# Last attention stage: the second pair's heads swap rows and key orders, the second pair's results move to a bank of their own, and the key-sum products move behind the next item's scores

## The chip, the cores and the metric

The kernel runs on one core of one Trainium2 chip. The metric is device time in microseconds (us) for one execution, lower is better. The engines are named as in the profile: PE is TensorE (matrix products and transposes), PEld its weight loads, DVE is VectorE, ACT is ScalarE, POOL is GpSimd, SP is SyncE. Each engine works through its own queue in order and waits on semaphores that the other engines raise.

## The reference, cut to what matters

The whole network is two layers on x of shape (2, 1024, 256): adapter, linear attention, mixture of experts, then sparse or dense attention, the attention that is changed here, an adapter and a feed-forward part. The changed part is local attention with 16 heads of 64 in blocks of 128 queries. A block sees its own block of keys and both neighbours (within 127 positions), and 64 "side" keys more, each the sum over 16 tokens of the input, projected:

```python
def _L1_attn_ref(x, Wq, Wk, Wv, Wo):        # x (2, 1024, 256); H, dh = 16, 64
    bl = 128; nb = L // bl; G = L // 16     # 8 blocks, 64 side keys
    q = einsum('bld,dhk->blhk', x, Wq) / sqrt(dh)
    k, v = einsum('bld,dhk->blhk', x, Wk), einsum('bld,dhk->blhk', x, Wv)
    g = einsum('bld,lg->bgd', x, one_hot(arange(L) // 16))
    side_k, side_v = einsum('bgd,dhk->bghk', g, Wk), einsum('bgd,dhk->bghk', g, Wv)
    k_cat = concat([3 blocks of k, side_k]); v_cat = concat([3 blocks of v, side_v])
    logits = einsum('bnqhd,bnkhd->bnhqk', qb, k_cat) + bias      # 0 or -1e9 outside |rel| <= 127
    m = maximum(logits.max(-1), 0)
    probs = exp(logits - m) / (exp(logits - m).sum(-1) + exp(-m))
    y = einsum('bnhqk,bnkhd->bnqhd', probs, v_cat)
    return einsum('blhk,hkd->bld', y, Wo)
```

## The kernel before, in words

Everything is float32. `attn1` handles the two sequences (b) one after the other. For each it computes the keys into `kT` (line 1577), 64 rows for the even head of a pair of heads and 64 rows for the odd one. The key blocks and the side keys stand in `kT` in an order that `KEYS` gives: `KEYS[0]` for the upper 64 rows, `KEYS[1]` for the lower 64. Then it computes the values (`v`) and the summed values (`sv`).

`attn1_heads` does the attention itself. Its unit is an item: one block n of 128 queries and two pairs of heads, m and m+1, so four heads. There are 8 blocks by 4, that is 32 items for a sequence, 64 in all. Blocks 0 and 7 are the edge blocks (two key blocks instead of three); the others are called inner here. An item passes five steps:

- `scores`: for each pair four products of 64 rows by 64 columns (two heads, two halves of the queries) into a tile `ps` of two banks. DVE merges the two neighbour blocks for an inner block (`copy_predicated`, lines 1691 and 1698: one copy of 128x128 and two of 64x64), then one instruction per head (1707) subtracts, masks and finds the extreme into `pe` and `nm`. ACT takes the exponentials in place (`exps`, 1726), pair 0 and pair 1 apart.
- `turn`: PE transposes `pe`, eight blocks into the banks `pt0` and `pt1` (1757) and two blocks with the side keys into `pts` (1758). Into the same `pts` go two transposes with the reciprocals of the item before (`recip`, 1737). ACT copies `pt0` (1763) and `pts` (1774) to SBUF, DVE copies `pt1` with its two masks (1765).
- `invert`: the reciprocal of the denominators (1742), widened by ACT (1744).
- `sums`: four products of the side weights with `sv` into `py` (1793), 64x64 each.
- `values`: twelve products (eight at an edge) of 128 rows by 64 columns into `py` (1810), accumulated on the sums. DVE then multiplies by the reciprocals into `yT` (1822).

`py` is one bank of four slots of 128 columns; an item uses two of them, the next item the other two. Queries for two blocks (`queries`, 1653) and the output product for two blocks (`output`, 1832) are interspersed, three and four times per sequence. The steps overlap: in round i the loop at line 1839 issues scores of item i, sums of item i-2, turn of item i-1, the second exponentials of item i, invert of i-1, and values of i-2. A scheduler sets the order in each engine's queue; `behind` adds an order between two instructions of one engine without a wait. PSUM's eight banks are all used: `ps` twice two, `pt0`, `pt1`, `pts`, `py`.

Of the kernel before, what the change touches and what calls it, by code (L numbers as in the profile page):

```python
# [18 lines left out]
P = 128  # L19
# [1496 lines left out]
def attn1(k, ci, x):  # L1516
# [7 lines left out]
    with tiles(tc, name="a1r", bufs=1) as rp:  # L1524
# [13 lines left out]
        for b in range(B):  # L1538
            kT = rp.tile([P, 8, S + 4 * (G + 2)], F32, name="kT")
            for i in range(2):  # L1540
                for at in KEYS[i].sums:
                    nc.gpsimd.memset(kT[64 * i : 64 * i + 64, :, at - 1 : at + G + 1 : G + 1], 0.0)
            v = rp.tile([P, NB, 1024], F32, name="v")

            sv = rp.tile([P, 2, 8, 64], F32, name="sv")
            with ExitStack() as st:
# [15 lines left out]
                for m in range(8):  # L1562
                    ms = slice(m * P, (m + 1) * P)
                    for half in range(2):
                        ts = slice(b * S + half * CK, b * S + (half + 1) * CK)
                        pq = pp.tile([P, CK], F32, name="pq", bufs=3)
                        for c in range(2):
                            nc.tensor.matmul(pq, lhsT=wk[:, c, ms], rhs=ci[:, c, ts], start=c == 0, stop=c == 1)  # L1568
                        gs = slice(half * G // 2, (half + 1) * G // 2)
                        nc.vector.reduce_sum(sk[:, m, gs], pq.rearrange("p (g t) -> p g t", t=16), axis=AX.X)  # L1570
                        for i in range(2):
                            hp = slice(64 * i, 64 * i + 64)
                            for n0, n1 in KEYS[i].runs(4 * half, 4 * half + 4):
                                at, w = KEYS[i].at[n0], (n1 - n0) * P
                                o = (n0 - 4 * half) * P
                                copy = nc.vector.tensor_copy if i else nc.scalar.copy
                                copy(kT[hp, m, at : at + w], pq[hp, o : o + w])
                    if beside:
                        next(beside[m // 4])
                    if m % 4 == 3:  # L1580
                        for i in range(2):
                            hp = slice(64 * i, 64 * i + 64)
                            for at in KEYS[i].sums:
                                nc.gpsimd.tensor_copy(kT[hp, m - 3 : m + 1, at : at + G], sk[hp, m - 3 : m + 1])
                for half in range(2):
                    hs = slice(half * CK, (half + 1) * CK)
                    for j in range(NB):
# [30 lines left out]
def attn1_heads(k, b, x, ci, kT, v, sv, masks, rp, sp, pp, yp):  # L1618
# [22 lines left out]
    def behind(ins, other):  # L1641

        how = mybir.DependencyInfo(mybir.DependencyClass.NoSync, mybir.DependencyReason.DATA)
        k.tc.add_manual_dep(ins.ins, other.ins.name, how, reason="order")

    def queries(n):

# [14 lines left out]
    def scores(it):  # L1662
# [2 lines left out]
            queries(0)  # L1665
        if m == 4 and n % 2 == 1 and n + 1 < NB:
            queries(n + 1)
        views = window(n)
# [4 lines left out]
        for pair in range(2):  # L1673
            ps = pp.tile([P, 2, CK], F32, name="ps")
            pe = sp.tile([P, 2, W], F32, name="pe", bufs=4)
            for half in range(2):
                qs = slice((n % 2) * P + half * 64, (n % 2) * P + half * 64 + 64)
                for hp, view in zip(hps, views):
                    c0, c1 = view.parts[half]
                    nc.tensor.matmul(  # L1680
                        ps[hps[half], view.head, c0:c1],
                        lhsT=rows["qT", n // 2, m // 4][hp, (m + pair) % 4, qs],
                        rhs=kT[hp, m + pair, view.start + c0 : view.start + c1],
                        start=True,
                        stop=True,
                    )
# [33 lines left out]

    def exps(it, pair):

        for view in window(it["at"][0]):
# [22 lines left out]
    def turn(it):  # L1746
        n, m = it["at"]

        pt = [yp.tile([P, 4, P], F32, name=f"pt{j}") for j in range(2)]
        pts = yp.tile([P, 2, 2, P], F32, name="pts")  # L1750
        for pair in range(2):
            pe = it["pe"][pair].rearrange("p i w -> p (i w)")
            for view in window(n):
                for j, block in enumerate(view.blocks):
                    at = view.place * (3 * P + 2) + j * P
                    to = pt[block != n] if inner(n) else pt[block != max(0, n - 1)]
                    nc.tensor.transpose(to[:, 2 * pair + view.head, :], pe[:, at : at + P], k.ident)  # L1757
            nc.tensor.transpose(pts[:, 0, pair, :], pe[:, 2 * P + 1 : 3 * P + 1], k.ident)  # L1758
        if it["no"]:
            recip(pts, it["no"] - 1)  # L1760
        ptt = it["pt"] = sp.tile([P, 3, 4, P], F32, name="ptt")
        its = it["pts"] = sp.tile([P, 2, 2, P], F32, name="ptts")
        nc.scalar.copy(ptt[:, 0], pt[0])
# [5 lines left out]
            )  # L1769
        else:  # L1770
            masked = nc.vector.tensor_copy(ptt[:, 1], pt[1])
        behind(masked, rows["least"])
        if it["no"]:
            rows["turned"] = nc.scalar.copy(its, pts)
        else:
            rows["turned"] = nc.scalar.copy(its[:, 0], pts[:, 0])

    def last():

        pts = yp.tile([P, 2, 2, P], F32, name="pts")  # L1780
        recip(pts, len(items) - 1)
        items[-1]["last"] = sp.tile([P, 2, 2, P], F32, name="ptts")
        nc.scalar.copy(items[-1]["last"][:, 1], pts[:, 1])

    py = yp.tile([P, 4, P], F32, name="py")

    def sums(it):
        n, m = it["at"]
        views = window(n)
        for pair in range(2):  # L1790
            for view in views:
                hs = slice(64 * view.place, 64 * view.place + 64)
                nc.tensor.matmul(  # L1793
                    py[64 * view.head : 64 * view.head + 64, (m + pair) % 4, :],
                    lhsT=sv[hs, views[0].place, m + pair, :],
                    rhs=it["pts"][hs, 0, pair, :],
                    start=pair == 0,
                    stop=False,
                    skip_group_check=True,
                )  # L1800

    def values(it):
        n, m = it["at"]
        k0 = max(0, n - 1)
        keys = [v[:, n], v[:, n - 1], v[:, n + 1]] if inner(n) else [v[:, k0], v[:, k0 + 1]]
        for pair in range(2):
            for j in range(len(keys)):
                for i in range(2):
                    hs = slice((2 * (m + pair) + i) * 64, (2 * (m + pair) + i) * 64 + 64)
                    nc.tensor.matmul(  # L1810
                        py[64 * i : 64 * i + 64, (m + pair) % 4, :],
                        lhsT=keys[j][:, hs],
                        rhs=it["pt"][:, j, 2 * pair + i, :],
                        start=False,
                        stop=j == len(keys) - 1,
                        skip_group_check=True,
                    )
        if n % 2 == 0 and m == 0:
            rows["yT"] = rp.tile([P, 8, 2 * P], F32, name="yT")
        ns = slice((n % 2) * P, (n % 2 + 1) * P)  # L1820
        after = it["last"] if it is items[-1] else items[it["no"] + 1]["pts"]
        nc.vector.tensor_mul(rows["yT"][:, m : m + 2, ns], py[:, m % 4 : m % 4 + 2], after[:, 1])
        if m == 6 and n % 2 == 1:
            output(n)

    def output(n):
        yT = rows["yT"]
# [297 lines left out]
```

## Time and profile before

| | us |
|---|---|
| timed runs, median of 3 | 1491.24 (1489.38 to 1491.75) |
| profiled execution, its own time | 1490.23 |
| its span, first to last instruction | 1488.5 |
| heads stage, first sequence | some 185 (945 to 1130 of the span) |
| heads stage, second sequence | some 190 (1228 to 1418) |
| mean granted TensorE clock | 0.959 |

The span counts from the first to the last instruction. Busy time of an engine is time with at least one instruction in flight, so matrix products that overlap count once. In the groups, "idle before" is the time for which the engine stood idle just before such an instruction, with what ended it. In the timeline a line is one instruction or a run of alike ones: start, duration, engine, line, operation, tiles, shape and count; a float32 product shows up as two passes, so that eight products are "x16".

### The profile page before, as it was taken

What the parts mean: (1) busy time and instruction counts of PE and PEld (TensorE: products, weight loads), DVE (VectorE), ACT (ScalarE), POOL (GpSimd) and SP (SyncE); (2) the same over time, 40 slices, a digit from 0 to 9 for tenths busy, and PEclk for the clock granted to TensorE, in tenths of its full rate; (3) what the DMA queues carried; (4) which work ended last, traced back from release to release, by engine and by line L of the source; (5) the groups of instructions that cost most, each with busy time, mean ns of one, the idle gap of its engine ahead of it and who ended that gap; (6) DMA issues with size and microseconds to landing.
All of it is one profiled execution on the core that took longest, in us unless ns stands there. A gap on an engine that the chain in (4) does not pass through costs nothing. (4 is left out here: it accounts for less than half of the span.)

```text
span 1488.5 us, 27374 instructions
## 1 busy us (share of the span) xinstructions
PE 1405.7 (94%) x10852; PEld 930.2 (62%) x10852; DVE 874.3 (59%) x2640; ACT 651.8 (44%) x1509; POOL 217.9 (15%) x201
## 2 busy tenths in 40 slices
PE   6998889999799999979999999999999999999998
PEld 3445877455556676656666644777776457777766
DVE  5545734121389942047787773577676637777674
ACT  3333242222222213207788832656564436556633
POOL 3333630022401632110000010000000200000011
PEclk9899678999889999989999999999999999999999
DMA  9600004300144343030000020000000000000001
GB/s 300 203 1 2 4 2 142 142 31 30 64 133 160 106 147 121 15 127 1 2 1 2 2 85 0 1 2 2 1 2 2 0 0 2 2 2 2 1 15 45
DMA packets 42759, 70.79 MB, mean 48 GB/s; under 512 B 7168, under 2 KB 35840, under 8 KB 39552
## 3 DMA queue, kind: packets, MB, share of 16 engines
q1 hardware_dynamic: 36576, 57.12, 11.4%
q0 software_dynamic: 3072, 8.65, 1.6%
q10 hardware_dynamic: 2976, 3.18, 0.7%
q8 instruction: 88, 1.44, 0.4%
q14 instruction: 47, 0.39, 0.1%
HBM read 45.09 MB, written 23.86 MB: 46 GB/s over the span
## 5 line engine op out<-in xcount | busy, mean ns | idle before, releaser
L1726 ACT ACTIVATE pe<-pe,nm 128x321 f32<-128x321 f32 x256 | 142.2, 559 | 109.2 <-DVE nm L1707 109.2
L1707 DVE CUSTOM_DVE_ANT_0 pe<-ps,wbs 128x321 f32<-128x321 f32 x256 | 114.8, 491 | 18.3 <-PE ps L1680 8.3
L1255 ACT ACTIVATE pe<-pe,nm 128x256 f32<-128x256 f32 x256 | 110.5, 498 | 19.6 <-DVE nm L1245 19.6
L988 PE MATMUL ph<-xt,w 128*128 128x512 f32 x256 | 114.3, 604 | 2.2 <-ACT xt L983 2.2
L996 PE MATMUL po<-w,h 128*128 128x256 f32 x512 | 111.8, 379 | 0.0
L996 PEld LDWEIGHTS po<-w,h 128*128 128x128 f32 x512 | 97.3, 190 | 16.6 <-issue 3.8
L1245 DVE CUSTOM_DVE_ANT_0 pe<-ps,lc 128x256 f32<-128x256 f32 x256 | 94.1, 417 | 19.1 <-PE ps L1229 18.2
L1680 PE MATMUL ps<-kT,qT 64*64 64x386 f32 (+3 forms) x1024 | 101.6, 490 | 3.2 <-ACT qT L1660 2.5
L918 DVE SCALAR_TENSOR_TENSOR lc<-iok,idx,lc 128x256 f32<-128x256 f32 x248 | 100.6, 500 | 0.0
L1810 PE MATMUL py<-ptt,v 128*64 128x128 f32 x1408 | 91.0, 277 | 0.0
L1000 POOL DMA_INDIRECT ys<-ye,row x32 | 63.0, 1970 | 180.4 <-DVE ye L999 160.7
L988 PEld LDWEIGHTS ph<-xt,w 128*128 128x128 f32 x256 | 48.6, 193 | 62.5 <-issue 55.9
L1810 PEld LDWEIGHTS py<-ptt,v 128*64 128x64 f32 x1408 | 75.5, 137 | 10.7 <-issue 10.7
L1757 PE MATMUL pt<-ident,pe 128*128 128x128 f32 x512 | 77.4, 280 | 0.0
L1264 PE MATMUL ptp<-ident,pe 128*128 128x128 f32 x512 | 73.0, 280 | 3.7 <-DVE pt L1268 3.0
L1264 PEld LDWEIGHTS ptp<-ident,pe 128*128 128x128 f32 x512 | 55.3, 141 | 30.9 <-ACT pe L1255 14.8
L991 ACT ACTIVATE h<-ph,vecs 128x512 f32<-128x512 f32 x64 | 44.0, 687 | 69.5 <-PE ph L988 69.5
L1757 PEld LDWEIGHTS pt<-ident,pe 128*128 128x128 f32 x512 | 56.8, 141 | 12.5 <-issue 10.0
L999 DVE TENSOR_TENSOR ye<-po,b 128x256 f32<-128x256 f32 x32 | 13.9, 434 | 79.2 <-PE po L996 79.2
L1680 PEld LDWEIGHTS ps<-kT,qT 64*64 64x64 f32 x1024 | 33.3, 132 | 42.1 <-issue 24.4
L1765 DVE TENSOR_TENSOR ptt<-pt,near 128x1024 f32<-128x1024 f32 x48 | 58.6, 1220 | 0.4 <-PE pt L1757 0.4
L671 PE MATMUL ph<-x,c2w 128*128 128x512 f32 (+2 forms) x160 | 58.4, 508 | 0.0
(365 smaller groups left out, 2674.3 us busy)
## 6 DMA issues: line engine op xcount, KB each, us to landing
w<-in_mw SPq DMA_DIRECT2D x16, 1024.0 KB, 5.0
xs<-z SPq DMA_DIRECT2D x8, 1088.0 KB, 12.0
ys<-z SPq DMA_DIRECT2D x4, 1024.0 KB, 11.3
xe<-xs SPq DMA_DIRECT2D x7, 544.0 KB, 7.2
more<-xs SPq DMA_DIRECT2D x7, 544.0 KB, 4.1
out_x<-o SPq DMA_DIRECT2D x8, 256.0 KB, 2.2
x<-in_xT SPq DMA_DIRECT2D x3, 512.0 KB, 6.3
wa<-in_wa SPq DMA_DIRECT2D x1, 1536.0 KB, 8.0
```

Of the source, the lines that this page charges most:

```text
L918: nc.vector.scalar_tensor_tensor(n, key, k.idx[:, qb, j : j + 1], n, ALU.is_equal, ALU.add)
L988: nc.tensor.matmul(ph, lhsT=w1[:, c, m * P : (m + 1) * P], rhs=xt[:, c, :], start=c == 0, stop=c == 1)
L996: nc.tensor.matmul(po, lhsT=h[:, m, j * P : (j + 1) * P], rhs=w2[:, m, :], start=m == 0, stop=m == 7)
L1000: nc.gpsimd.indirect_dma_start(out=rows[e * 4 + j], out_offset=bass.IndirectOffsetOnAxis(ap=row[:, j : j + 1], axis=0), in_=ye[:, j, :], i ...
L1245: nc.vector.tensor_tensor_reduce(out=pe[:, j, :], in0=it["ps"][i][:, j, :], in1=k.lc[:, q0 + j, :], scale=-1.0, scalar=3.0e38, op0=ALU.add ...
L1255: nc.scalar.activation(pe[:, j, :], pe[:, j, :], AF.Exp, bias=nm, scale=-1.0)
L1264: nc.tensor.transpose(ptp[:, kb, j, :], it["pe"][i][:, j, kb * P : (kb + 1) * P], k.ident)
L1680: nc.tensor.matmul(ps[hps[half], view.head, c0:c1], lhsT=rows["qT", n // 2, m // 4][hp, (m + pair) % 4, qs], rhs=kT[hp, m + pair, view.sta ...
L1707: rows["least"] = nc.vector.tensor_tensor_reduce(out=pe[:, j], in0=ps[:, i, view.used : view.used + W], in1=wbs[:, o : o + W], scale=-1.0, ...
L1726: e = nc.scalar.activation(part, part, AF.Exp, bias=it["nm"][:, col], scale=-1.0, accum_out=it["den"][:, col])
L1757: nc.tensor.transpose(to[:, 2 * pair + view.head, :], pe[:, at : at + P], k.ident)
L1810: nc.tensor.matmul(py[64 * i : 64 * i + 64, (m + pair) % 4, :], lhsT=keys[j][:, hs], rhs=it["pt"][:, j, 2 * pair + i, :], start=False, sto ...
```

## The change

For the second pair of an item (odd m) the two heads swap their key orders: its even head uses `KEYS[1]` and its odd head `KEYS[0]`, and in `pe` they swap places. So pair 0's key-sum products use the array's quadrants upper rows and left columns, lower rows and right columns (or the reverse), and pair 1's the two other quadrants. The filling of `kT` follows: the same copies with other blocks, and twice as many memsets and POOL copies of the side keys, each half the size.

`py` and `pts` are replaced by one tile `both` of two banks. The first bank holds two slots of pair 0's results and the two side-weight transposes; the second holds the two reciprocal transposes and two slots of pair 1's results. The four transposes together are called `turned`; they are copied by one ACT instruction as before.

The accumulation is turned round: the values start it and the sums end it. The sums of an item move one round later, behind the scores of item i in round i, where i-3 is the item; so do the multiplication into `yT`, now one instruction per pair of heads and ordered behind the masked copy, and the output product. The first score product is ordered behind the last value product of the round before.

```diff
-def window(n):
+def window(n, pair):
     first = 0 if n == 0 or n in (1, 3, 5) else 1
-    return [KEYS[i].view(i, n, first ^ i) for i in range(2)]
+    return [KEYS[i ^ pair].view(i, n, first ^ i ^ pair) for i in range(2)]
...
-                for at in KEYS[i].sums:
-                    nc.gpsimd.memset(kT[64 * i : 64 * i + 64, :, at - 1 : at + G + 1 : G + 1], 0.0)
+                for pair in range(2):
+                    for at in KEYS[i ^ pair].sums:
+                        nc.gpsimd.memset(kT[64 * i : 64 * i + 64, pair::2, at - 1 : at + G + 1 : G + 1], 0.0)
...
-                            for n0, n1 in KEYS[i].runs(4 * half, 4 * half + 4):
-                                at, w = KEYS[i].at[n0], (n1 - n0) * P
+                            keys = KEYS[i ^ (m % 2)]
+                            for n0, n1 in keys.runs(4 * half, 4 * half + 4):
+                                at, w = keys.at[n0], (n1 - n0) * P
...
-                            for at in KEYS[i].sums:
-                                nc.gpsimd.tensor_copy(kT[hp, m - 3 : m + 1, at : at + G], sk[hp, m - 3 : m + 1])
+                            for pair in range(2):
+                                ms = slice(m - 3 + pair, m + 1, 2)
+                                for at in KEYS[i ^ pair].sums:
+                                    nc.gpsimd.tensor_copy(kT[hp, ms, at : at + G], sk[hp, ms])
...
+                    if "product" in rows:
+                        behind(product, rows.pop("product"))
...
-    def recip(pts, no):
+    def recip(no):
...
-            nc.tensor.transpose(pts[:, 1, pair, :], rdw, k.ident)
+            nc.tensor.transpose(turned[:, 1, pair, :], rdw, k.ident)
...
-        pts = yp.tile([P, 2, 2, P], F32, name="pts")
...
-            nc.tensor.transpose(pts[:, 0, pair, :], pe[:, 2 * P + 1 : 3 * P + 1], k.ident)
+            nc.tensor.transpose(turned[:, 0, pair, :], pe[:, 2 * P + 1 : 3 * P + 1], k.ident)
...
-        behind(masked, rows["least"])
+        rows["masked"] = behind(masked, rows["least"])
...
-            rows["turned"] = nc.scalar.copy(its, pts)
+            rows["turned"] = nc.scalar.copy(its, turned)
...
-    py = yp.tile([P, 4, P], F32, name="py")
+    both = yp.tile([P, 8, P], F32, name="py")
+    py = [both[:, 0:2], both[:, 6:8]]
+    turned = both[:, 2:6].rearrange("p (k pair) q -> p k pair q", k=2)
 
     def sums(it):
...
                 nc.tensor.matmul(
-                    py[64 * view.head : 64 * view.head + 64, (m + pair) % 4, :],
+                    py[pair][64 * view.head : 64 * view.head + 64, it["no"] % 2, :],
                     lhsT=sv[hs, views[0].place, m + pair, :],
                     rhs=it["pts"][hs, 0, pair, :],
-                    start=pair == 0,
-                    stop=False,
+                    start=False,
+                    stop=True,
...
+        for pair in range(2):
+            y = nc.vector.tensor_mul(rows["yT"][:, m + pair, ns], py[pair][:, it["no"] % 2], after[:, 1, pair])
+            behind(y, rows["masked"])
+        if m == 6 and n % 2 == 1:
+            output(n)
 
     def values(it):
...
-                    nc.tensor.matmul(
-                        py[64 * i : 64 * i + 64, (m + pair) % 4, :],
+                    rows["product"] = nc.tensor.matmul(
+                        py[pair][64 * i : 64 * i + 64, it["no"] % 2, :],
...
-                        start=False,
-                        stop=j == len(keys) - 1,
+                        start=j == 0,
+                        stop=False,
...
-        nc.vector.tensor_mul(rows["yT"][:, m : m + 2, ns], py[:, m % 4 : m % 4 + 2], after[:, 1])
-        if m == 6 and n % 2 == 1:
-            output(n)
...
-    for i in range(len(items) + 2):
-        for j, step in ((0, scores), (2, sums), (1, turn), (0, late), (1, invert), (2, values)):
+    for i in range(len(items) + 3):
+        for j, step in ((0, scores), (3, sums), (1, turn), (0, late), (1, invert), (2, values)):
             if 0 <= i - j < len(items):
                 step(items[i - j])
-            elif step is turn and i:
+            elif step is turn and i == len(items) + 1:
                 last()
```

More of the change, by code (lines that the diff above doesn't have):

```diff
@@ L1644, in behind @@
         k.tc.add_manual_dep(ins.ins, other.ins.name, how, reason="order")
+        return ins
     def queries(n):
@@ L1667, in scores @@
             queries(n + 1)
-        views = window(n)
         hps = [slice(64 * i, 64 * i + 64) for i in range(2)]
@@ L1673, in scores @@
         for pair in range(2):
+            views = window(n, pair)
             ps = pp.tile([P, 2, CK], F32, name="ps")
@@ L1679, in scores @@
                     c0, c1 = view.parts[half]
-                    nc.tensor.matmul(
+                    product = nc.tensor.matmul(
                         ps[hps[half], view.head, c0:c1],
@@ L1721, in exps @@
     def exps(it, pair):
-        for view in window(it["at"][0]):
+        for view in window(it["at"][0], pair):
             col = slice(2 * pair + view.head, 2 * pair + view.head + 1)
@@ L1749, in turn @@
         pt = [yp.tile([P, 4, P], F32, name=f"pt{j}") for j in range(2)]
-        pts = yp.tile([P, 2, 2, P], F32, name="pts")
         for pair in range(2):
             pe = it["pe"][pair].rearrange("p i w -> p (i w)")
-            for view in window(n):
+            for view in window(n, pair):
                 for j, block in enumerate(view.blocks):
@@ L1757, in turn @@
                     nc.tensor.transpose(to[:, 2 * pair + view.head, :], pe[:, at : at + P], k.ident)
-            nc.tensor.transpose(pts[:, 0, pair, :], pe[:, 2 * P + 1 : 3 * P + 1], k.ident)
+            nc.tensor.transpose(turned[:, 0, pair, :], pe[:, 2 * P + 1 : 3 * P + 1], k.ident)
         if it["no"]:
-            recip(pts, it["no"] - 1)
+            recip(it["no"] - 1)
         ptt = it["pt"] = sp.tile([P, 3, 4, P], F32, name="ptt")
@@ L1771, in turn @@
             masked = nc.vector.tensor_copy(ptt[:, 1], pt[1])
-        behind(masked, rows["least"])
+        rows["masked"] = behind(masked, rows["least"])
         if it["no"]:
-            rows["turned"] = nc.scalar.copy(its, pts)
+            rows["turned"] = nc.scalar.copy(its, turned)
         else:
-            rows["turned"] = nc.scalar.copy(its[:, 0], pts[:, 0])
+            rows["turned"] = nc.scalar.copy(its[:, 0], turned[:, 0])
     def last():
-        pts = yp.tile([P, 2, 2, P], F32, name="pts")
-        recip(pts, len(items) - 1)
+        recip(len(items) - 1)
         items[-1]["last"] = sp.tile([P, 2, 2, P], F32, name="ptts")
-        nc.scalar.copy(items[-1]["last"][:, 1], pts[:, 1])
-    py = yp.tile([P, 4, P], F32, name="py")
+        nc.scalar.copy(items[-1]["last"][:, 1], turned[:, 1])
+    both = yp.tile([P, 8, P], F32, name="py")
+    py = [both[:, 0:2], both[:, 6:8]]
+    turned = both[:, 2:6].rearrange("p (k pair) q -> p k pair q", k=2)
     def sums(it):
         n, m = it["at"]
-        views = window(n)
         for pair in range(2):
+            views = window(n, pair)
             for view in views:
@@ L1793, in sums @@
                 nc.tensor.matmul(
-                    py[64 * view.head : 64 * view.head + 64, (m + pair) % 4, :],
+                    py[pair][64 * view.head : 64 * view.head + 64, it["no"] % 2, :],
                     lhsT=sv[hs, views[0].place, m + pair, :],
                     rhs=it["pts"][hs, 0, pair, :],
-                    start=pair == 0,
-                    stop=False,
+                    start=False,
+                    stop=True,
                     skip_group_check=True,
                 )
+        if n % 2 == 0 and m == 0:
+            rows["yT"] = rp.tile([P, 8, 2 * P], F32, name="yT")
+        ns = slice((n % 2) * P, (n % 2 + 1) * P)
+        after = it["last"] if it is items[-1] else items[it["no"] + 1]["pts"]
+        for pair in range(2):
[3 more added lines that the diff above has]
+            output(n)
     def values(it):
@@ L1809, in values @@
                     hs = slice((2 * (m + pair) + i) * 64, (2 * (m + pair) + i) * 64 + 64)
-                    nc.tensor.matmul(
-                        py[64 * i : 64 * i + 64, (m + pair) % 4, :],
+                    rows["product"] = nc.tensor.matmul(
+                        py[pair][64 * i : 64 * i + 64, it["no"] % 2, :],
                         lhsT=keys[j][:, hs],
                         rhs=it["pt"][:, j, 2 * pair + i, :],
-                        start=False,
-                        stop=j == len(keys) - 1,
+                        start=j == 0,
+                        stop=False,
                         skip_group_check=True,
                     )
[L1818 to L1822, printed above, removed]
-        if m == 6 and n % 2 == 1:
-            output(n)
     def output(n):
```

## The prediction

> **What bounds the kernel now.** I read the page first, then busy time in the two heads stages, the chain of waits, and the timeline of one ordinary round.
>
> ```profile
> span 1488.5 us, 27374 instructions
> PE 1405.7 (94%) x10852; PEld 930.2 (62%) x10852; DVE 874.3 (59%) x2640; ACT 651.8 (44%) x1509; POOL 217.9 (15%) x201
> ```
>
> ```profile
> core 0: us, PE busy (x) PEld busy (x) DVE busy (x) ACT busy (x) POOL busy (x), PEclk, DMA share, GB/s
> 1228.00:1418.00 190.00, 189.19 (x1973) 144.89 (x1973) 134.84 (x474) 117.39 (x340) 1.30 (x1) 1.00 0.01 2
> 1308.00:1324.00 16.00, 16.00 (x204) 12.06 (x204) 14.96 (x53) 11.71 (x37) 0.00 (x0) 1.00 0.01 3
> ```
>
> The changed stage fills PE to over 99% at a granted clock of 1.00. Over three ordinary rounds DVE is 94% busy too, so it has little to spare. The chain of waits, in order of time, shows one round of 4.8 us as PE alone:
>
> ```profile
> 1310.04 1.46 PE ps L1680 x16
> 1311.50 0.44 PE py L1793 x8
> 1311.94 0.59 PE pt L1757 x4
> ...
> 1313.40 1.46 PE py L1810 x24
> 1314.86 1.46 PE ps L1680 x16
> ```
>
> The key-sum products (L1793) are 0.44 us of it. The timeline gives the spacing between engines, which I need for the changed round:
>
> ```profile
> 1309.97 1.53 PE L1680 MATMUL ps<-kT,qT 64*64 64x386 f32 x16
> 1310.92 0.30 DVE L1691 COPY_PREDICATED ps<-near,ps 128x128 f32<-128x128 uint8 x1 [0.29 <-PE ps L1680]
> 1312.61 0.29 DVE L1691 COPY_PREDICATED ps<-near,ps 128x128 f32<-128x128 uint8 x1
> 1312.93 0.49 DVE L1698 COPY_PREDICATED ps<-near,ps 64x64 f32<-64x64 uint8 x2
> 1313.95 0.58 ACT L1774 COPY ptts<-pts 128x512 f32<-128x512 f32 x1
> 1315.51 0.39 DVE L1822 TENSOR_TENSOR yT<-py,ptts 128x256 f32<-128x256 f32 x1
> 1315.96 0.55 PEld L1793 LDWEIGHTS py<-ptts,sv 64*64 64x64 f32 x8 [0.32 <-DVE yT L1822]
> ```
>
> The last two lines matter most. The sums at 1315.96 write two slots of `py`, and the `yT` instruction before them reads the two other slots. Yet PE waits until `yT` ends (1315.90). Waits here go by bank, not by slot. In the waits of the second heads stage:
>
> ```profile
> PEld py L1793 <- DVE yT L1822: 6.1, 15, 0.7
> ```
>
> Today this is nearly free, since `pts` has a bank of its own and `yT` is normally early.
>
> **What the change removes.** Eight passes of 128 columns, two at a time, cost 0.44 us. The scores run four at a time: 16 passes of 386 columns in 1.46 us, 0.95 ns a column for a group of four. Two groups of four over 128 columns give 0.24 us. So 0.20 us per item, 64 items: 13 us of PE time, if nothing else came up.
>
> **What it adds on PE's path.** The built program's order for an ordinary round shows, with the engine waited for:
>
> ```
> scores x4, scores x4 [DVE], sums x4
> 6 transposes into pt0/pt1
> L1764 turned x2 [DVE]
> L1744 reciprocal transposes x2 [ACT]
> L1763 two pt0 transposes of the next item [ACT]
> L1826 values x12 [ACT]
> ```
>
> Matching the semaphore values, the DVE instruction behind `turned` is the second `yT` half of this same round. The ACT instruction behind the values is this same round's copy of `turned`. Both follow from the shared banks. DVE's order is: pair 0's merge and two reductions, pair 1's 128x128 copy, first `yT` half, a 64x64 copy, second `yT` half. So `yT` stands behind pair 0 of the scores just issued. That closes a loop through all three engines, each round:
>
> - Scores issued to DVE's first copy: 0.95 (1309.97 to 1310.92).
> - DVE on pair 0: 1.69 (1310.92 to 1312.61).
> - Pair 1's copy to the end of the second `yT` half. No row has a half. From below 0.63: 0.33 from this copy to the next (1312.61 to 1312.93), 0.10 for another instruction, 0.20 for a half of L1822's 0.39. From above 1.30: the same 0.33, 0.31 for a `yT` half as long as a whole one (start to start), 0.27 for a 64x64 copy (half of the 0.53 that two take), 0.39. I take 0.85: the first half hides in the 0.33 that the next copy waits for its predecessor anyway, then 0.27 and 0.25.
> - DVE's end to PE: 0.06 (1315.90 to 1315.96).
> - Four transposes to the last result: 0.70. Three of them (L1758, two L1737) took 0.59, from 1312.80 to 1313.39; one more spaced 0.11.
> - PE's end to ACT: 0.09, at the stage's tail (L1737 ends 1416.63, L1783 starts 1416.72).
> - ACT copies `turned`: 0.58 (L1774).
> - ACT's end to PE: 0.05 (queries: L1660 ends 1305.75, scores load 1305.80).
> - Values until the next scores: 1.46 (chain).
>
> Sum 6.43 against 4.81 us, so +1.62. The ends of the `yT` term make it 6.21 to 6.88.
>
> ACT is not later than this. It does both exponentials of pair 0 and the copy of `pt0` first, and today the next copy starts 3.98 after the scores (1313.95). The loop has it start at 4.34. Queued behind the copy on ACT are pair 1's exponentials; they end about 6 us into the round and are wanted in the next one. Behind `yT` on DVE stand pair 1's reductions and the masked copy, done about 5.8 into the round. DVE's extra instruction, 0.2 us at most, then lies in idle time.
>
> **Sum over one sequence.** 24 items are inner blocks. Before, their rounds with three queries and three outputs took 161.4 us (scores at 1234.04 to those at 1395.47).
>
> - 18 rounds without filler, at 6.43, one of them with eight instead of twelve values (-0.44): 115.3.
> - Three query rounds. The scheduler puts two query products (0.44 each, 7.1/16) before `turned` and two after. They start when pair 0's `ps` comes free at about 2.70, and end 3.59; four transposes, ACT and values as above end at 6.47; the other twelve take 5.33. That is 11.80 (one -0.44): 35.0 against 11.9 each before, so these rounds lose nothing.
> - Three output rounds. The output (7.1) runs from 2.70 to 9.80, then eight transposes (0.98 and 0.16 to land), 0.09, 0.58, 0.05, 1.46: 13.12, together 39.4.
>
> That is 189.7, or +28.3. At the edges DVE's order has `yT` behind all four reductions: 0.83 (1400.07 to 1400.90), 1.66, 0.16 and 0.25 for `yT`, 0.06, 0.70, 0.09, 0.58, 0.05, and 1.02 for eight values: 5.40 against 4.15, +1.25. Five rounds: +6.2. The first rounds and the drained tail, with one round more: about +1. Per sequence +35.5, for two +71.
>
> **What costs nothing.** POOL's doubled memsets and copies: 28 copies of 0.40 become 56 of half the size, and the 5.6 us more in a half at worst lie beside the projection of the values (32 products of L1591, over 14 us); if that cover were gone, up to 11 us in all. The `kT` copies on ACT and DVE only change blocks. No DMA is moved.
>
> The profiled execution took 1490.2, 1.0 below the median. 1490.2 + 71 + 1 gives 1562.
>
> **A rule beside the rows.** The row is the wait of L1793 on L1822, though the slots differ: 15 times in this stage. The Trainium skill, "PSUM — Partial Sum Buffer", section "PSUM bank collisions raise a hardware error", says why: two engines on one bank and the same 32 partitions collide even at different columns, so accesses are to be kept apart by bank and quadrant. It speaks against putting `turned` beside `py`: with it both waits stand and the sum is 1562. If waits went by columns, both would go, and PE's saving alone would give 1478.
>
> **Rivals.**
>
> 1. *Both waits close the loop* (forecast): 1562. Own range 1548 to 1580: the ends of the `yT` term (-0.22, +0.45) over 36 rounds are -8 and +16.
> 2. *Only one closes it*: say the values find the copy of `turned` done. Then a round is 0.95+1.69+0.85+0.06, six transposes 0.73, values 1.46: 5.74, +0.93. 36 rounds give +33, edges and outputs about +8: 1532. Against it: `turned` cannot be copied before it is written. With the ACT wait alone it is 3.98+0.58+0.05+1.46 = 6.07, +1.26: about 1548.
> 3. *Faster*: `yT` and ACT are always early and PE saves 0.20 per item: 1478. It decides if `yT` lands before PE reaches `turned`, about 2.4 us after the scores. DVE ends pair 0 of these scores only at 2.64. A gain for the path needs a DVE order unlike the built one. The same would hold if the change did not reach the chip as built: 1491.
> 4. *The clock falls as well*: PE would be about 70% busy in an ordinary round. In this trace 690 to 705 us has PE 93% busy at clock 1.00, but 405 to 420, at 48%, has 0.50. At 0.8 the PE parts of the loop (0.95, 0.70, 1.46) grow by 0.78, 36 rounds 28 us, and query and output rounds some 15: 1605. Idle pieces of about a microsecond speak against it.
>
> **How the numbers follow.** Forecast 0.72, one wait only 0.12, clock 0.10, faster 0.04, no change 0.02. For 8 in 10 the range is 1530 to 1590: the forecast's own, the one-wait case, and half-way to the clock case. Within 0.2% (3 us, about what can be told here from no change) 0.02, faster 0.04, slower 0.94.
>
> **What would show it.** Right: ordinary rounds near 6.4 us; PE's longest waits in the heads on DVE `yT` (by L1764) and on ACT's copy of `turned` (by L1826), about 1 and 0.6 us a round; the sums in 0.2 to 0.3 us; DVE and ACT with idle time instead of 94%; heads stages near 220 us; clock 1.00. Wrong: rounds near 4.6 with PE still full, or a `yT` that runs ahead of pair 0.

## The result and the profile after

The changed kernel takes 1570.97 us (median, 1566.11 to 1573.20) where the kernel before takes 1489.60 us (1488.38 to 1491.75) on the same chip: a ratio of 1.0539 with a 95% interval of 1.0520 to 1.0557. It is slower by 81 us. The forecast was 1562 with a range of 1530 to 1590.

The head of the page, and two stretches of busy time (the second heads stage, and some five rounds of the first one):

```profile
span 1568.4 us, 27383 instructions
PE 1403.0 (89%) x10852; PEld 908.3 (58%) x10852; DVE 878.9 (56%) x2704; ACT 654.5 (42%) x1509; POOL 193.0 (12%) x243
```

```profile
core 0: us, PE busy (x) PEld busy (x) DVE busy (x) ACT busy (x) POOL busy (x), PEclk, DMA share, GB/s
1264.00:1490.00 226.00, 188.80 (x1926) 136.37 (x1926) 136.70 (x506) 117.62 (x340) 1.31 (x1) 1.00 0.01 1
1040.00:1072.00 32.00, 26.08 (x269) 19.02 (x265) 20.48 (x75) 14.14 (x44) 0.00 (x0) 1.00 0.01 2
```

PE, DVE and ACT are busy for about as long as before (PE 1403.0 against 1405.7 us), POOL for less (193.0 against 217.9), and the span is 79.9 us longer. So it is not more work; the engines wait more. PE fell from 99.6% of the second heads stage to 84%, at a granted clock of 1.00 as before.

The chain of waits over one ordinary round (start, duration, what) is the same question as the chain shown of before, where it was PE alone:

```profile
1041.16 0.85 PE ps L1685 x8
...
1043.81 0.21 DVE ps L1698
1044.02 0.19 DVE yT L1813
1044.21 0.13 DVE ps L1705
1044.34 0.20 DVE yT L1813
...
1044.59 0.44 PE py L1764 x2
...
1045.33 0.60 ACT ptts L1780
...
1045.97 1.53 PE py L1826 x24
```

It now goes round: scores on PE, pair 0 and the two `yT` halves on DVE, the turned transposes on PE, their copy on ACT, the values on PE, and the next scores. In the waits of the second heads stage (us in total, times, longest) the two crossings stand as two lines of their own:

```profile
PEld py L1764 <- DVE yT L1813: 25.1, 21, 1.8
PEld py L1826 <- ACT ptts L1780: 16.2, 29, 0.7
```

Where the 79.9 us lie, in the second sequence: the 24 inner items take 193.1 us against 161.4 (scores of the first to scores of the first edge item behind them), +31.7; the first four items +2.6; the last three edge rounds +4.1; from the last scores to the addition of the output +1.9. That is 40.2. The same four stretches of the first sequence give 40.4, and the rest of the program is 0.7 shorter.

### The profile page after: what moved, and what is told of

It reads as the page before. It is cut to its first block, busy times and chain, and to the rows that moved or that the text cites. A ratio compares the mean times of both kernels' runs of the same rounds, so it can differ in the third digit from the quotient of the medians.

```text
span 1568.4 us, 27383 instructions
## 1 busy us (share of the span) xinstructions
PE 1403.0 (89%) x10852; PEld 908.3 (58%) x10852; DVE 878.9 (56%) x2704; ACT 654.5 (42%) x1509; POOL 193.0 (12%) x243
## 5 line engine op out<-in xcount | busy, mean ns | idle before, releaser
L996 PEld LDWEIGHTS po<-w,h 128*128 128x128 f32 x512 | 97.3, 190 | 16.6 <-issue 3.8
L1698 DVE COPY_PREDICATED ps<-near,ps 128x128 f32<-128x128 uint8 x96 | 28.3, 295 | 111.2 <-PE ps L1685 110.5
L1763 PE MATMUL pt<-ident,pe 128*128 128x128 f32 x512 | 83.2, 283 | 7.2 <-ACT ptt L1769 6.6
L1841 PE MATMUL ps<-yT,w1ao 128*128 128x256 f32 x256 | 59.8, 384 | 8.0 <-DVE nm L1714 3.9
L1764 PE MATMUL py<-ident,pe 128*128 128x128 f32 x128 | 28.4, 291 | 40.0 <-DVE yT L1813 40.0
L1658 PE MATMUL ps<-c,w1aq 128*128 128x256 f32 x256 | 59.6, 383 | 1.9 <-DVE nm L1714 1.9
L1000 POOL DMA_INDIRECT ys<-ye,row x32 | 34.4, 1076 | 208.4 <-DVE ye L999 188.0
```

What stands on the lines that cost most here:

```text
L996: nc.tensor.matmul(po, lhsT=h[:, m, j * P : (j + 1) * P], rhs=w2[:, m, :], start=m == 0, stop=m == 7)
L1658: nc.tensor.matmul(pq[:, i, :], lhsT=wq[:, c, (m + i) * P : (m + i + 1) * P], rhs=ci[:, c, b * S + n * P : b * S + (n + 2) * P], start=c == 0,
L1841: nc.tensor.matmul(po[:, c, 0 : 2 * P], lhsT=wo[:, m, c * P : (c + 1) * P], rhs=yT[:, m, :], start=m == 0, stop=m == 7)
```

## The experiments

**1. The swap undone.** Only the second pair's rows and key orders go back; banks and order stay.

```diff
-    return [KEYS[i ^ pair].view(i, n, first ^ i ^ pair) for i in range(2)]
+    return [KEYS[i].view(i, n, first ^ i) for i in range(2)]
...
-                            keys = KEYS[i ^ (m % 2)]
+                            keys = KEYS[i]
```

> The changed kernel with one part undone: the second pair keeps the first pair's rows and key order, so its key-sum products use the same two quadrants as the first pair's and take 0.44 us an item again instead of 0.24. Order and banks stay as changed. My theory (the round is a loop over scores, vector engine, yT, transposes, ACT copy, values, all of it made by the two shared banks): the sums run while PE waits for yT, so nothing is on the path; rounds stay at 6.3 to 6.8 and the time at 1571, within 4 us. Rival (the sums are on PE's path, the 13 us of the forecast are real and only outweighed): 0.20 more in each of 64 rounds, 1584.

Measured: 1575.05, ratio to before 1.0574 (1.0551 to 1.0597), some 4 to 5 us above the changed kernel. The rival's 1584 is a ratio of 1.063 and lies outside the interval, so the four quadrants are not worth 13 us here; whether they are worth a few or none, these runs do not decide. The saving itself is real in the timeline: the sums take 0.33 us from their first product to the next transpose in the changed kernel, 0.55 with the swap undone and before (1311.32 to 1311.87). The changed kernel, then the swap undone:

```profile
1042.44 0.40 PE L1800 MATMUL py<-ptts,sv 64*64 64x128 f32 x8
1042.77 0.88 PE L1763 MATMUL pt<-ident,pe 128*128 128x128 f32 x6
```

```profile
1315.84 0.62 PE L1800 MATMUL py<-ptts,sv 64*64 64x128 f32 x8
1316.39 0.88 PE L1763 MATMUL pt<-ident,pe 128*128 128x128 f32 x6
```

PE spends what it saves waiting for `yT`: the inner items of the first sequence take 193.1 us in the changed kernel and 193.4 with the swap undone. In this profile the second sequence takes 195.1, of which 1.4 lie in two rounds with a short fall of the granted clock (last section). The rounds shift between the blocks (6.45 in 2 and 4, 6.60 to 6.68 in most of 3 and 5), for the reason that experiment 6 shows.

**2. The banks undone too.** On top of experiment 1, both pairs' results in one bank and the turned transposes in a bank of their own. What is left of the change is the order.

```diff
-    both = yp.tile([P, 8, P], F32, name="py")
-    py = [both[:, 0:2], both[:, 6:8]]
-    turned = both[:, 2:6].rearrange("p (k pair) q -> p k pair q", k=2)
+    both = yp.tile([P, 4, P], F32, name="py")
+    py = [both[:, 0:2], both[:, 2:4]]
+    turned = yp.tile([P, 2, 2, P], F32, name="pts")
```

> The changed order alone: no swap, the results of both pairs in one bank of four slots and the four transposes in a bank of their own as before, but the sums after the next scores, yT in two halves, the values first, one round more per sequence. My theory (the shared banks are what costs): the transposes wait for no yT and the values for no ACT copy; rounds of 4.8 to 5.1 (the second half of yT adds some 0.2 us to a vector engine that was 94% busy), one more round per sequence, 1490 to 1510, I take 1498. Rival (the order itself costs, because yT now stands behind pair 0 of the next scores and the values wait for it in their bank): yT ends 3.3 to 3.9 after the scores, PE reaches the values at 3.4, so up to 0.5 a round or 1515; if it stayed near 1570, the banks would have nothing to do with it.

Measured: 1504.54, ratio 1.0093 (1.0068 to 1.0119). So in this order the shared banks carry some 66 of the 81 us, and the order by itself some 15. The waits of the turned transposes for `yT` and of the values for ACT's copy are gone. One remains, in the timeline of one round (start, duration, engine and line, then the idle time before it):

```profile
1273.40 0.27 DVE L1813 TENSOR_TENSOR yT<-py,ptts 128x128 f32<-128x128 f32 x1
1273.73 1.29 PEld L1826 LDWEIGHTS py<-ptt,v 128*64 128x64 f32 x24 [0.43 <-DVE yT L1813]
```

The values write the bank that `yT` reads, and `yT` stands behind pair 0: from the scores 0.96 to DVE, 1.80 for pair 0, 0.80 to the end of `yT`, 0.06, and 1.46 for the values are 5.08, the round measured there. The rival named for this run was right in part: the late `yT` costs by itself, 0.27 in this round (4.81 before); other blocks have rounds of 5.03 to 5.51. In the last block the rounds are back at 4.59, 4.60 and 4.16.

**3. The first wait taken away.** In the changed kernel, `yT` is ordered between pair 0's merge copies and its reductions (and pair 1's merge copies behind those).

```diff
+            if pair == 0 and it["no"] > 2:
+                sums(items[it["no"] - 3])
             for view in views:
...
                 rows["least"] = nc.vector.tensor_tensor_reduce(
...
+                if pair == 0 and it["no"] > 2:
+                    behind(rows["least"], rows["y"])
```

> The changed kernel with the two halves of yT placed on the vector engine between the merge copies of pair 0 and its reductions, instead of behind pair 0; banks, swap and order on PE as changed. My theory (two waits in a row): the first goes, since yT then ends 2.30 after the scores (0.95 + 0.80 for the merges + 0.55) and PE reaches the turned transposes at 2.36. The copy of the transposes still stands behind pair 0's two exponentials on ACT, which the 0.55 us on the vector engine put back: copy at 4.06, end 4.64, + 0.05 + 1.46 for the values = 6.15 a round against 6.33 to 6.82. Some 0.4 us in 36 rounds: 1555, between 1545 and 1562. Rival (the wait for yT is the whole cost): 5.2 a round, 1520 or less.

Measured: 1557.99, ratio 1.0459 (1.0427 to 1.0490). Of the turned transposes' waits for `yT` one of 0.3 us is left in the second heads stage. Ordinary rounds are 6.14 to 6.46, and 7.17 to 7.27 behind the queries, where the changed kernel has 6.40 to 6.89. One round: scores at 1392.08, ACT's copy at 1396.14 (4.06 later, as summed) behind pair 0's second exponential, values at 1396.76, next scores at 1398.22. So taking one wait away alone gives back 13 us of 81: the other is nearly as late.

**4. Both waits taken away as far as the order allows.** As 3, and pair 0's exponentials are ordered behind the copy on ACT (`early` is these exponentials).

```diff
-            if pair and it["no"]:
+            if it["no"]:
                 behind(e, rows["turned"])
...
-        for j, step in ((0, scores), (1, turn), (0, late), (1, invert), (2, values)):
+        for j, step in ((0, scores), (1, turn), (0, early), (0, late), (1, invert), (2, values)):
```

> As early_yT, and ACT copies the four transposes ahead of pair 0's exponentials. My theory: PE reaches the turned transposes at 2.36, ends them at 3.01, + 0.09, ACT 0.58, + 0.05, values 1.46: 5.19 a round; the vector engine needs about the same, 4.9 + 0.25. That is 0.4 above the 4.81 of before in 36 rounds, 1 us in ten edge rounds and one round more per sequence: 1520, between 1505 and 1535. Rival (something other than these two waits holds the round): above 1545.

Measured: 1522.21, ratio 1.0203 (1.0173 to 1.0233). Ordinary rounds are 5.38 to 5.66 (6.09 to 6.19 behind the queries) instead of 5.19, since ACT's copy of `pt0` stands in front of the copy of the turned transposes (1311.35 and 1311.93 in one round). The values' wait for ACT's copy is longer than in experiment 3, where PE had already stood 26.9 us at two transposes that wait for pair 0's exponentials. From 1280 to 1480 us, 3 and then 4:

```profile
PEld pt L1774 <- ACT pe L1744: 26.9, 40, 1.2
...
PEld py L1838 <- ACT ptts L1791: 7.0, 21, 0.3
```

```profile
PEld py L1837 <- ACT ptts L1790: 19.4, 21, 1.1
```

**5. `yT` in one instruction**, the two banks read with a step between them.

```diff
-        for pair in range(2):
-            y = nc.vector.tensor_mul(rows["yT"][:, m + pair, ns], py[pair][:, it["no"] % 2], after[:, 1, pair])
-            behind(y, rows["masked"])
+        y = nc.vector.tensor_mul(rows["yT"][:, m : m + 2, ns], both[:, it["no"] % 2 : 8 : 6], after[:, 1])
+        behind(y, rows["masked"])
```

> The changed kernel with yT in one instruction over both banks, so that no 64x64 copy stands between two halves. By the loop the stretch from pair 1's first copy to the end of yT becomes 0.20 + 0.41 = 0.61 instead of 0.81 or 1.09, in all blocks alike: rounds of 6.13 and 6.24 (with pair 0 at 1.69 and 1.80) instead of 6.33 and 6.72, 36 rounds of -0.35 and edges unchanged: 1557, between 1552 and 1563. If the loop did not run through yT's end, the rounds would stay and so would 1571.

Measured: 1556.88, ratio 1.0447 (1.0409 to 1.0484); rounds of 6.10 in blocks 3 and 5 and 6.22 in 2 and 4. They are 0.23 and 0.50 shorter, where 0.20 and 0.48 were summed: the end of `yT` is on the loop.

**6. Why some blocks are slower.** In the changed kernel ordinary rounds take 6.33 to 6.41 in blocks 3, 5 and 6, 6.72 in 2 and 4, and 6.8 to 6.9 in 1 (6.38 where a round has eight values instead of twelve). The blocks differ in which half of the rows the 64x64 merge copies work on. Two orders of these copies were run. First, rows 0 to 63 first in both pairs:

```diff
-                for i in range(2):
+                for i in sorted(range(2), key=lambda i: -kinds[i]):
                     rs = slice(64 * (1 - kinds[i]), 64 * (1 - kinds[i]) + 64)
```

> The changed kernel with one thing turned round: of a pair's two 64x64 merge copies the one on rows 0 to 63 stands first on the vector engine wherever there is one. In the changed kernel the rounds of blocks 3, 5 and 6 take 6.33 to 6.41 and those of 1, 2 and 4 take 6.72 to 6.89; in the latter pair 1's first 64x64 copy, which stands between the two halves of yT, works on rows 64 to 127. If those rows are the reason (the copy then starts only when the yT half before it has ended, 0.32 after its start instead of 0.20, and the second half 0.27 after the copy instead of 0.13), the rounds of blocks 2 and 4 fall from 6.72 to 6.35, six ordinary and two output rounds a sequence, 6 us in all: 1566. Block 1 has no copy on rows 0 to 63 and stays. Rival (something else of these blocks): rounds and time unchanged, 1571.

Measured: 1569.92, ratio 1.0547 (1.0516 to 1.0578). Blocks 2 and 4 fell to 6.45, but blocks 3 and 5 rose to 6.45 to 6.52: the expectation had only half of the effect. Second, rows 64 to 127 first in pair 0 and rows 0 to 63 first in pair 1:

```diff
-                for i in range(2):
+                for i in sorted(range(2), key=lambda i: kinds[i] * (1 - 2 * pair)):
                     rs = slice(64 * (1 - kinds[i]), 64 * (1 - kinds[i]) + 64)
```

> The changed kernel with the 64x64 merge copies put in the order that the fast blocks have: pair 0 rows 64 to 127 first, pair 1 rows 0 to 63 first, in every block that has both. With rows 0 to 63 first in both pairs the rounds of blocks 2 to 5 were all 6.45 to 6.52: yT's stretch was short (0.81) in all of them, and pair 0 long (1.80 instead of 1.69). If each pair's order acts on its own, blocks 2 and 4 fall from 6.72 to 6.33 and blocks 3 and 5 stay at 6.33; six ordinary rounds a sequence at 0.39 make 1566, within 4 us. If the order is not the cause, 6.72 stays.

Measured: 1567.10, ratio 1.0532 (1.0499 to 1.0564), and rounds of 6.33 to 6.34 in blocks 2 to 5 (6.40 behind the queries). Block 1 has no copy on rows 0 to 63, and its rounds stay at 6.8 to 6.9 (outside the stretch of lower clock that the last section names). The time as a whole cannot tell 4 us; the rounds can: the inner items of the first sequence take 190.7 us instead of 193.1. In the timeline of DVE, a round of block 4 of the changed kernel and then one of block 2, whose copies work on the same rows, in this one:

```profile
1050.17 0.30 DVE L1698 COPY_PREDICATED ps<-near,ps 128x128 f32<-128x128 uint8 x1
1050.38 0.28 DVE L1813 TENSOR_TENSOR yT<-py,ptts 128x128 f32<-128x128 f32 x1
1050.70 0.24 DVE L1705 COPY_PREDICATED ps<-near,ps 64x64 f32<-64x64 uint8 x1
1050.97 0.29 DVE L1813 TENSOR_TENSOR yT<-py,ptts 128x128 f32<-128x128 f32 x1
```

```profile
1333.56 0.29 DVE L1698 COPY_PREDICATED ps<-near,ps 128x128 f32<-128x128 uint8 x1
1333.76 0.28 DVE L1813 TENSOR_TENSOR yT<-py,ptts 128x128 f32<-128x128 f32 x1
1333.96 0.21 DVE L1705 COPY_PREDICATED ps<-near,ps 64x64 f32<-64x64 uint8 x1
1334.09 0.28 DVE L1813 TENSOR_TENSOR yT<-py,ptts 128x128 f32<-128x128 f32 x1
```

A 64x64 copy on rows 0 to 63 starts 0.20 after the `yT` half in front of it, one on rows 64 to 127 only when that half has ended (0.32), and the next half 0.27 instead of 0.13 after that. The same shows between the pairs: where pair 0's last copy was on rows 64 to 127, pair 1's first copy starts 0.11 later, behind the end of the reductions. A copy on the other rows also works on other columns, and the two orders do not part rows from columns.

**7. The same banks, another order of their users.** Scores of item i, values and sums of i-2, the transposes into `pt0` and `pt1` of i-1, then the four turned transposes; the reciprocals are now those of the same item, and no round is added.

```diff
-        for j, step in ((0, scores), (3, sums), (1, turn), (0, late), (1, invert), (2, values)):
+        for j, step in ((0, scores), (1, turn), (2, ends), (0, late)):
...
+            if pair and it["no"]:
+                invert(items[it["no"] - 1])
+            if pair and it["no"] > 1:
+                results(items[it["no"] - 2])
             for view in views:
...
-            recip(it["no"] - 1)
+        recip(it["no"])
...
-        after = it["last"] if it is items[-1] else items[it["no"] + 1]["pts"]
+        after = it["pts"]
```

Here `results` is `values` and then `sums`, and `ends` is the output.

> Banks, swap and four quadrants as changed, but the users of the two banks put in another order: scores of item i, values and sums of i-2, the transposes into pt0 and pt1 of i-1, then the four turned transposes of i-1, the reciprocals now of the same item; yT halves on the vector engine between pair 1's merge copies and its reductions. My theory (it is the order of the banks' users that costs, not the sharing itself): the copy of the transposes lies beside the scores, the wait for yT beside the pt transposes; PE needs 1.46 + 1.46 + 0.24 + 0.88 + 0.60 = 4.6 a round, but the vector engine 1.69 + 1.68 + 1.14 + 0.08 + 0.50 = 5.1, which then sets the round, like the rounds of 5.07 with a bank of its own. No round more. 36 rounds of +0.3 and 64 sums of at most -0.2 at the edges alone: 1498, between 1488 and 1510. Rival (any sharing closes a loop of about 6 us): 1550 or more.

Measured: 1487.91, ratio 0.9989 (0.9972 to 1.0006): the loss is gone, with the swap and the shared banks still there. It is just under the range that was expected. Two ordinary rounds and the start of a third, which has queries; then the middle of a round in the timeline:

```profile
core 0: us, PE busy (x) PEld busy (x) DVE busy (x) ACT busy (x) POOL busy (x), PEclk, DMA share, GB/s
1286.00:1302.00 16.00, 15.96 (x190) 10.97 (x188) 15.43 (x57) 12.24 (x36) 0.00 (x0) 1.00 0.00 1
```

```profile
1343.13 0.45 PE L1803 MATMUL py<-ptts,sv 64*64 64x128 f32 x8
1343.52 0.98 PE L1776 MATMUL pt<-ident,pe 128*128 128x128 f32 x7
...
1343.87 0.47 DVE L1816 TENSOR_TENSOR yT<-py,ptts 128x128 f32<-128x128 f32 x2
...
1344.40 0.33 PE L1777 MATMUL py<-ident,pe 128*128 128x128 f32 x1
...
1345.24 0.59 ACT L1791 COPY ptts<-py 128x512 f32<-128x512 f32 x1
```

The copy on ACT (1345.24) lies beside the next scores (from 1345.09), and `yT` beside the transposes into `pt0` and `pt1`. PE is full (15.96 of 16.00 us) and DVE nearly so (15.43), so my expectation that DVE alone would set the round, at 5.1, was not right. And yet the round is 4.88, not the 4.6 summed for PE. From the first score product to the first transpose without the values it is 1.46 + 0.39 = 1.85, against 1.35 + 0.33 = 1.68 in the changed kernel and 1.35 + 0.55 = 1.90 before: with the sums between products of other shapes only 0.05 is left of what the four quadrants save. Then the first turned transpose comes 0.06 after `yT` ends (1344.34) and the transposes take 1.57 instead of 1.46.

**8. One `yT` instruction in that order**, as in 5.

> As reorder, with yT in one instruction over both banks instead of two halves. If the vector engine sets the round there, this takes 0.2 off it (0.31 start to start instead of 0.50): rounds of 4.8 to 4.9, 1490, between 1482 and 1498: what the four quadrants save on PE (0.20 a round, 13 us) still does not show. If PE sets it: 4.6 a round in both, 1480.

Measured: 1492.75, ratio 1.0019 (0.9994 to 1.0043), rounds of 4.88 to 5.03. It gains nothing, which fits with PE full; the scheduler also put the first turned transpose two places earlier, where it waits for `yT` (some 0.2 in one round).

**9. Work taken off DVE in that order.** One half of the masked copy goes over ACT to POOL, and POOL widens the reciprocals.

```diff
-            masked = nc.vector.tensor_mul(
-                ptt[:, 1:3],
...
+            nc.scalar.copy(ptt[:, 1], pt[1])
+            nc.gpsimd.tensor_mul(ptt[:, 1], ptt[:, 1], nearf[:, 0:1].to_broadcast([P, 4, P]))
+            masked = nc.vector.tensor_mul(ptt[:, 2], pt[1], near[:, 1:2].to_broadcast([P, 4, P]))
```

> As reorder_one, with work taken off the vector engine: of the masked copy of pt1 (1.14 a round) it does one half (about 0.6), ACT copies the other half (0.56) and POOL multiplies it (1.09 for 128x512 in the profile); POOL also widens the reciprocals (0.40 off ACT). The vector engine then needs some 4.3, ACT 4.1, POOL 1.5, PE 4.6. If the vector engine is what hides PE's saving, the round becomes PE's 4.6: 13 us under before, 1478, between 1470 and 1486. If not, or if POOL and the vector engine slow each other, 1490 or more.

Measured: 1503.74, ratio 1.0088 (1.0058 to 1.0118), where 1478 was hoped for. The waits from 1280 to 1420 us, a part of the second heads stage, show new ones:

```profile
DVE ptt L1787 <- ACT ptt L1785: 16.8, 20, 1.1
PEld py L1828 <- ACT ptts L1791: 9.2, 15, 0.8
PEld py L1828 <- POOL ptt L1786: 5.8, 10, 0.7
```

DVE's half waits for ACT's copy, which reads the same bank and writes another part of the same tile, and the values wait for ACT's copy of the turned transposes and for POOL's product (1.27 in one round, 1.09 expected). How much each of these waits costs was not run apart.

**10. An order that keeps the sums beside products of their shape.** Values of i-2, scores of pair 0 of item i, sums of i-2, scores of pair 1, turned transposes of i-1, transposes into `pt0` and `pt1` of i-1. The core of the edit, on top of 8:

```diff
+        if it["no"] > 1:
+            values(items[it["no"] - 2])
         for pair in range(2):
...
+            if pair == 0 and it["no"] > 1:
+                sums(items[it["no"] - 2])
+        if it["no"]:
+            side(items[it["no"] - 1])
```

> Banks, swap and quadrants as changed, in an order made to hide both waits and to keep the sums beside products of their own shape: values of i-2, scores of pair 0 of item i, sums of i-2, scores of pair 1, turned transposes of i-1, transposes into pt0 and pt1, again values. yT in one instruction, ahead of pair 0's merge copies. yT lies beside the scores of pair 1 (0.73), the copy of the transposes beside the pt transposes (0.90). In the reordered kernel the sums cost 0.38 on PE although four ran at once, with another shape before and behind them; here 0.24 is expected, PE 4.7 a round. The vector engine has 4.7 to 4.9. 1484, between 1478 and 1494. If the chain exponentials, reciprocal, widening, transposes does not close in time, PE waits for ACT by the reciprocal transposes and it is 1500 or more.

Measured: 1634.18, ratio 1.0976 (1.0950 to 1.1001), the slowest of all, where 1484 was expected. The waits from 1280 to 1420 us, a part of the second heads stage:

```profile
PEld py L1840 <- ACT ptt L1794: 20.7, 12, 1.9
PEld py L1840 <- DVE ptt L1796: 9.1, 7, 1.4
PEld py L1774 <- DVE yT L1829: 8.4, 12, 1.2
```

The wait of the turned transposes (L1774) for `yT` got shorter but did not go, and I had opened another: the values now follow at once on the transposes whose copies they read, so PE waits for `pt0`'s copy, which stands behind pair 0's exponentials on ACT, and for the masked copy, which stands behind all reductions on DVE. The sums do cost 0.22 between scores of their own shape (1357.32 to 1357.54), as expected. The waits are not all of the 143 us: over the two heads stages the granted clock stood at 0.50 in 20 stretches, 72 us together. If all of that was PE's own work at half speed, up to some 36 us (an estimate) are the clock's.

## Why the prediction was right

**The loop.** It was named with its crossings between engines and its sum, and the chain of waits shows it. Its terms, forecast and measured (a fast round from 1041.09, a slow one from 1047.42):

| term | forecast | fast | slow |
|---|---|---|---|
| scores to DVE's first copy | 0.95 | 0.95 | 0.95 |
| DVE on pair 0 | 1.69 | 1.69 | 1.80 |
| pair 1's copy to the end of `yT` | 0.85 | 0.81 | 1.09 |
| DVE to PE | 0.06 | 0.05 | 0.05 |
| four transposes | 0.70 | 0.65 | 0.66 |
| PE to ACT, copy, ACT to PE | 0.72 | 0.72 | 0.72 |
| values | 1.46 | 1.46 | 1.46 |
| round | 6.43 | 6.33 | 6.73 |

Experiments 3, 4, 5 and 6 show that the loop runs through these places: each term that they shorten comes back in the round as summed, except for ACT's copy of `pt0` in experiment 4.

**The sum.** 18 ordinary rounds: 115.3 forecast, 117.8 measured. Three query rounds: 35.0 and 35.9. Three output rounds: 39.4 and 39.4. The edges, first rounds and tail: +7 forecast, +8.6 measured, of which the tail is 1.9, where about 1 was taken for it and the first rounds. Per sequence that is +35.5 against +40.2. The step that was mis-sized most is the `yT` term with the one before it: taken as 0.85 behind 1.69 everywhere, where half of the inner blocks (1, 2 and 4) have 1.09 behind 1.80 or close to it, and the others a little less than was taken, so that the two misses partly cancel (1.09 lies inside the bounds of 0.63 to 1.30; the 1.80 was not bounded at all). The cause is the order of the copies on the two row halves, experiment 6. The Trainium skill, "VectorE: DVE Perf Modes", section "Two Vector instructions with no wait between them", has a model that I did not use: an instruction whose input or output starts in another group of 32 partitions than the last one that read or wrote that memory starts only when all earlier ones have ended. The two orders of experiment 6 agree with it in both places: 0.28 between the two `yT` halves, 0.11 at the step from pair 0 to pair 1.

**What was removed.** 0.20 a round forecast, 0.22 measured (0.55 to 0.33), and hardly any of it reaches the time, as forecast: PE waits for `yT` either way, and undoing it (experiment 1) costs some 4 to 5 us instead of 13.

**The rivals.** "Only one wait" was forecast in two forms. The ACT wait alone is experiment 3: 6.07 a round and about 1548 forecast, 6.14 to 6.46 and 1557.99 measured, which is short of 1571. The `yT` wait alone, forecast at 5.74 and 1532, was not run; against it stands the changed kernel's own profile, where the values wait for ACT's copy 29 times in the second heads stage. "The clock falls" did not come: it stayed at 1.00 in both heads stages though PE idles 16% of the second. It was no idle rival, since the clock did fall in experiment 10. "Faster" needed a DVE order unlike the built one; experiment 3 has `yT` that early and is still 69 us above the kernel before, since the wait for ACT's copy stays.

**The rule on banks.** The waits of the turned transposes for `yT` and of the values for ACT's copy go by bank, though the columns differ, as the rule cited in the prediction says. I read it as speaking against `turned` beside `py`. Experiment 7 narrows that: the same banks cost nothing measurable in an order where other work stands between one user and the next.

**Hidden work.** POOL's doubled memsets and copies stayed hidden: from the last scores of the first sequence to the first of the second it is 97.1 us instead of 95.2, and the drained tail in that stretch (18.4 us from the last scores to the addition of the output, 16.6 before) accounts for the 1.9.

## What to carry to other kernels

When a buffer moves into a bank that another engine still reads, write down every user of that bank in each engine's order, and add up the way round: what counts is how long each user stands behind unrelated work on its own in-order engine, not how long it takes. Cover for such a wait is work that stands between the two users on the waiting engine, and an order that covers one pair may bring two other dependent steps side by side, as experiment 10 did. A saving on an engine that will wait anyway is worth little or nothing, so price the wait first.

## What the runs showed of the hardware that was not expected

- On DVE the half of the rows that a 64x64 copy works on goes with whether it, and the next instruction, overlap the one in front: 0.20 against 0.32 from start to start, 0.13 against 0.27 for the next, and 0.11 at the step from one pair to the other.
- Four small products at a time were cheap only beside products of their own shape: scores and sums together took 1.68 us with the sums right behind the scores, 1.85 with the values between them. The Trainium skill, "TensorEngine Tiling (Array Packing)", section "Key Properties", says that a change of the tiling mode drains the engine. The 0.17 came with one change of shape more in a round; that the drain is its cause was not tested.
- The granted clock can fall inside a busy stage. In the profiled run of the second order of experiment 6 it was 0.50 from 1302.5 to 1305.9 us, in the middle of a stage otherwise at 1.00, and two rounds took 1.6 us more together. Such stretches last 3.4 us (one lasts 6.8). Besides the 20 of experiment 10, the heads stages have two in the first order of experiment 6, one each in experiments 1 and 5, and none in the changed kernel. In the 3.4 us before such a stretch (1299.1 to 1302.5 in the second order of experiment 6) PE was busy for 20 to 49% in 24 of the 25 cases and for 61% in that of experiment 5; the changed kernel's heads stages, cut into pieces of this length, have none under 54%. Three pieces of 45 to 48% in experiment 10 were not followed by a fall. So the clock goes with PE's idle time just before, but no run was made to test it.
